# One of four additions of the negated row maxima, in an attention that runs beside another layer, put on GpSimd

## The chip, the cores and the metric

The kernel runs on one core of a Trainium2 chip. It is one launch, and the metric is the device time of that launch in microseconds. All arithmetic is float32. The engines are called by their short names: PE is TensorE (PEld its weight loads), DVE is VectorE, ACT is ScalarE, POOL is GpSimd and SP is SyncE. In this kernel every DMA of the main part is issued from SP.

## What is computed

The input is `x` of shape (4, 64, 64, 256). Layer 0 is a gated block: layernorm, a projection to 768 channels, two selective scans over 2x2 windows, a depthwise 3x3 convolution with a pointwise product, a gate, an output product, and a feed-forward part. Layer 1 is self-attention over the 4096 tokens of each of the four images:

```
f = xf @ Wf + bf
g = xf @ Wg + bg
hh = xf @ Wh + bh
scores = jnp.einsum('bnd,bmd->bnm', g, f)
attn = jax.nn.softmax(scores, axis=-1)
o = jnp.einsum('bnm,bmc->bnc', attn, hh)
o = o @ Wo + bo
out = gamma * o + xf
```

The change touches the softmax alone: the subtraction of the row maximum ahead of the exponential.

## The kernel before

**Two layers side by side.** Layer 0 is cut into 32 blocks of 512 tokens (4 images of 8 blocks). It runs alone until the first image is through (`until(NBLK - 1)`), since attention needs all keys and values of an image. From there on attention on the images that are ready runs beside the rest of layer 0, as Python generators whose pieces are interleaved by hand. `fill(RATE)` lets layer 0 advance by 7.2 "us" of the costs that its generators yield, and it is called once per step of attention. When layer 0 is through, the remaining queries are treated by other functions, `late_weights` and `attend_late`, which the change doesn't touch.

**Layer 0 on the vector engine.** The scan is most of it. For each direction and each of 8 states, L470 or L474 multiplies a PSUM bank (the transposed decays of L462) with SBUF data, L492 makes the next state from two SBUF tiles, and L485 adds to the output from two SBUF tiles. The convolution's taps (L595) and the layernorm (`layernorm`, L291 to L306) are on the vector engine too. Layernorm sends two small operations through GpSimd (L300, L301), and L303 waits for the second. In `tail` GpSimd adds a row of biases to `xo`, four times 128x256 (L660). These and a few memsets are all that GpSimd does.

**Attention beside it.** A block is 128 queries. `weights` makes its softmax weights in nine steps, each ended by a `yield`:

1. scores of half of the keys into four PSUM banks (L844), copied by ACT into two `eq` tiles of 128x1024 (L852);
2. the running maximum over them, DVE (L858, L860);
3. the scores of the other half, two more `eq` tiles;
4. the rest of the maximum (L860, L863);
5. two PE transposes, a DVE reduction with negation (L869), a PE transpose and an ACT copy (L873), which leave the negated maxima of the 128 queries in every partition of `nb`, 128x128;
6. to 9. for each of the four `eq` tiles `es[0]` to `es[3]`: an addition of `nb`, repeated eight times along the tile (L877), and an exponential in place on ACT (L878).

`attend` runs a block's products with the values, eight steps of four matmuls (L1036). In each step it advances `own` (the weights of its own block, if some are left), then `beside` (the weights of the next block), then layer 0. Eight steps advance `beside` through its steps 1 to 8, so step 9, the tile with `n == 3`, is left over: it is issued as `own` after the first step of the following `attend`. Step `k` of `attend` reads `es[k // 2]`, so `es[3]` is first read in step 6.

**Order.** A scheduler turns this order into one instruction stream per engine and puts in the semaphores. Each engine then works in the order of its own stream. The four `eq` tiles of a block come from a pool of six buffers, `nb` from a pool of two.

The lines concerned: the additions L877 and the exponentials L878; L873, which writes `nb`; L660, L300 and L301, which share GpSimd; L470, L474, L485, L492, L595, L860 and L303, which share the vector engine.

Of the kernel before, what the change touches and what calls it, by code (L numbers as in the profile page):

```python
# [23 lines left out]
ALU = mybir.AluOpType  # L24
# [4 lines left out]
P = 128  # L29
# [30 lines left out]
def block_then_attention_kernel(  # L60
# [18 lines left out]
    nc = tc.nc  # L79
# [85 lines left out]
    def behind(ins, last):  # L165

        if last is not None:
            tc.add_manual_dep(
                ins.ins, last.ins.name,
                mybir.DependencyInfo(mybir.DependencyClass.NoSync, mybir.DependencyReason.DATA), reason="side by side",  # L170
            )
        return ins
# [3 lines left out]
    def aside(shape=(P, TOK)):  # L176

        i = turn[0]
        turn[0] = (i + 1) % 4
        return pss.tile(list(shape), F32, tag=f"q{i}", name=f"q{i}")  # L180

    def four():

        return [
            pss.tile([P, TOK], F32, tag=f"q{i}", name=f"q{i}") for i in ((turn[0] - 1 - r) % 4 for r in range(4))
        ]
# [644 lines left out]
    def weights(b, q, es):  # L831


        fQ, gq = quarters[b], gqs.pop((b, q))
        mx = one.tile([P, TOK], F32, tag="mx", name="mx")
        for g in range(2):
            pr = four()

            with tc.high_priority():
                last = None  # L840
                for s in range(4):
                    at = g * TOK + s * P
                    for r in range(4):
                        ins = nc.tensor.matmul(  # L844
                            pr[r][:, s * P : (s + 1) * P], lhsT=fQ[CK * r : CK * (r + 1), at : at + P],
                            rhs=gq[CK * r : CK * (r + 1), :], start=True, stop=True,
                        )
                        last = behind(ins, last)
            for a in range(2):
                e = ep.tile([P, 2, TOK], F32, tag="eq", name="eq")  # L850
                for j in range(2):
                    nc.scalar.copy(e[:, j, :], pr[2 * a + j])  # L852
                es.append(e)
            yield
            for r in range(4):
                e = es[2 * g + r // 2]
                if g == 0 and r == 0:
                    nc.vector.tensor_tensor(mx, e[:, 0, :], e[:, 1, :], ALU.max)  # L858
                elif g == 1 or r > 1:
                    nc.vector.tensor_tensor(mx, mx, e[:, r % 2, :], ALU.max)  # L860
            if g == 0:
                yield
        nc.vector.tensor_tensor(mx[:, :QB], mx[:, :QB], mx[:, QB:], ALU.max)  # L863
        yield
        pm = aside()
        for c in range(2):
            nc.tensor.transpose(pm[:, c * P : (c + 1) * P], mx[:, c * P : (c + 1) * P], ident)
        nm = st.tile([P, 1], F32, tag="nm", name="nm")
        nc.vector.tensor_reduce(nm, pm[:, :QB], AX.X, ALU.max, negate=True)  # L869
        pn = aside()  # L870
        nc.tensor.transpose(pn[:, :P], nm.to_broadcast([P, P]), ident)
        nb = two.tile([P, P], F32, tag="nb", name="nb")
        nc.scalar.copy(nb, pn[:, :P])  # L873
        yield
        for n, e in enumerate(es):
            e8 = e.rearrange("p r (s q) -> p (r s) q", s=4)
            nc.vector.tensor_tensor(e8, e8, nb.unsqueeze(1).broadcast_to([P, 8, P]), ALU.add)  # L877
            nc.scalar.activation(e, e, AF.Exp)  # L878
            yield

# [180 lines left out]
    for n in range(4):  # L1061
        load_values(0, 0, n)
    es = []
    own = weights(0, 0, es)
    for _ in own:
        fill(RATE)
    a = 0
    while True:
        b, q = divmod(a, NQ)
        b1, q1 = divmod(a + 1, NQ)  # L1070
        if q1 == 0:
            until((b1 + 1) * NBLK - 1)
        ahead = []
        late = ready["tail"] == LAST - 1 and q1 % 2 == 0
        if late:
            n0 = (b1, q1 // 2)
            load_late_queries(*n0)
            beside = twice(late_weights(*n0, 0, ahead))
            attend(b, q, es, own, beside, lambda n: load_late_values(*n0, n))
            es = ahead  # L1080
            break
        if q1 == 0:
            quarter(b1, one, "fQ")
        load_queries(b1, q1)
        beside = weights(b1, q1, ahead)
        attend(b, q, es, own, beside, lambda n: load_values(b1, q1, n))
        es, own = ahead, beside
        a += 1
# [100 lines left out]
```

## Time and profile before

| what | value |
|---|---|
| runs (median of 3) | 5259.01 us (5250.38 to 5259.54) |
| the profiled execution | 5265.47 us |
| its span in the profile | 5263.6 us |
| granted TensorE clock, mean | 0.978 |
| layer 0 alone | until about 900 us |
| attention beside layer 0 | about 900 to 4330 us, 74 query blocks |
| attention alone (late functions) | about 4330 us to the end |
| L877 | 296 instructions, 357.4 us, 1220 ns each |
| GpSimd, all of it | 304 instructions, 204.0 us |

A block beside layer 0 takes about 47 us, so a step of `attend` takes about 6 us. The span of 5263.6 us is what the rows of the profile add up against. The profiled execution's own time is 1.9 us longer, and it lies 6.5 us above the median of the runs.

In the rows of the profile, "busy" is the time in which an engine executes, and "idle before" is how long the engine stood still just ahead of such instructions, with what ended the wait. Ends of matmuls are modelled, and spans on GpSimd are rough.

### The profile page before, as it was taken

Reading aid. Unit: us, or ns where it says so; the run is one execution under the profiler, and the core shown is the slowest. Engines: PE = TensorE matmul, PEld = TensorE weight load, DVE = VectorE, ACT = ScalarE, POOL = GpSimd, SP = SyncE. Lnnn points to the kernel's source line nnn. Section 1 sums busy time; section 2 is a strip of 40 time slices with the busy share of each in tenths; the row PEclk is TensorE's granted clock in tenths of the full one; section 3 lists DMA queues with packets and bytes.
Section 4 is the critical chain, followed back from the end, with each engine's and each line's share of the span. In section 5 each row is a group of like instructions: output and inputs, shape, how many; then the busy total and the mean of one; then the engine's idle time right before and its main releaser. Section 6 shows DMA issues by size and latency. Waiting matters only on the chain. (4 is left out here: it accounts for less than half of the span.)

```text
span 5263.6 us, 76327 instructions
## 1 busy us (share of the span) xinstructions
PE 4955.8 (94%) x27138; PEld 3543.4 (67%) x27138; DVE 4517.3 (86%) x8256; ACT 3571.5 (68%) x5489; POOL 204.0 (4%) x304
## 2 busy tenths in 40 slices
PE   7999998999999999999999999999999999999999
PEld 4565565666666666666666666666666667888887
DVE  7999999999899988998989988898989866666665
ACT  6778778667777767677777767777777635555554
POOL 0000000000000000000000000000000000000000
PEclk8999999999999999999999999999999999999999
DMA  1010011333333333334333333333333344444444
GB/s 48 26 44 19 23 34 34 102 122 115 118 104 119 113 109 115 114 116 118 118 111 106 119 108 111 118 114 118 112 116 104 112 129 146 147 147 147 147 147 139
DMA packets 330284, 554.14 MB, mean 105 GB/s; under 512 B 51504, under 2 KB 85936, under 8 KB 329904
## 3 DMA queue, kind: packets, MB, share of 16 engines
q1 hardware_dynamic: 326384, 545.40, 34.2%
q8 instruction: 214, 3.51, 0.3%
q10 hardware_dynamic: 3520, 3.87, 0.2%
q14 instruction: 166, 1.36, 0.1%
HBM read 490.28 MB, written 58.79 MB: 104 GB/s over the span
## 5 line engine op out<-in xcount | busy, mean ns | idle before, releaser
L1036 PE MATMUL acc<-vt,eq 128*128 128x257 f32 x4736 | 1215.4, 392 | 17.2 <-issue 7.6
L406 ACT ACTIVATE e<-dt,a_sc 128x384 f32<-128x384 f32 x1536 | 853.3, 611 | 272.8 <-PE bank L462 262.5
L1036 PEld LDWEIGHTS acc<-vt,eq 128*128 128x128 f32 x4736 | 875.0, 195 | 234.2 <-issue 107.6
L462 PEld LDWEIGHTS bank<-ident,e 128*128 128x128 f32 x4320 | 521.2, 143 | 319.5 <-issue 113.4
L462 PE MATMUL bank<-ident,e 128*128 128x128 f32 x4320 | 658.9, 279 | 79.1 <-DVE p L474 37.1
L1014 PE MATMUL bank<-vt,eT 128*128 128x257 f32 x2560 | 645.8, 382 | 0.0
L492 DVE SCALAR_TENSOR_TENSOR h<-u,bc,p 128x384 f32<-128x384 f32 x1024 | 613.4, 613 | 0.4
L485 DVE SCALAR_TENSOR_TENSOR y<-h,bc,y 128x384 f32<-128x384 f32 x960 | 589.0, 614 | 3.2 <-ACT y L483 0.4
L474 DVE TENSOR_TENSOR p<-bank,h 128x384 f32<-128x384 f32 x960 | 517.1, 548 | 55.1 <-PE bank L462 54.5
L1014 PEld LDWEIGHTS bank<-vt,eT 128*128 128x128 f32 x2560 | 478.6, 189 | 83.7 <-issue 13.9
L852 ACT COPY eq<-q 128x512 f32<-128x512 f32 x592 | 308.6, 587 | 192.6 <-PE q L844 117.5
L948 DVE TENSOR_TENSOR mx<-mx,eT 128x512 f32<-128x512 f32 x378 | 261.7, 692 | 152.2 <-ACT eT L943 121.3
L878 ACT ACTIVATE eq<-eq 128x1024 f32<-128x1024 f32 x296 | 308.1, 1053 | 103.0 <-DVE eq L877 100.1
L877 DVE TENSOR_TENSOR eq<-eq,nb 128x1024 f32<-128x1024 f32 x296 | 357.4, 1220 | 7.6 <-ACT nb L873 7.4
L595 DVE SCALAR_TENSOR_TENSOR ydw<-xp,vec,ydw 128x512 f32<-128x512 f32 x496 | 357.8, 743 | 1.4
L943 ACT COPY eT<-q 128x512 f32<-128x512 f32 x432 | 221.5, 597 | 194.7 <-PE q L935 194.7
L860 DVE TENSOR_TENSOR mx<-mx,eq 128x512 f32<-128x512 f32 x444 | 306.5, 690 | 38.4 <-ACT eq L852 31.5
L406 ACT ACT_TABLE_LOAD x241 | 309.2, 1283 | 14.4 <-PE bank L462 10.2
L485 DVE SCALAR_TENSOR_TENSOR y<-p,bc,y 128x384 f32<-128x384 f32 x512 | 313.1, 612 | 0.4
L470 DVE SCALAR_TENSOR_TENSOR p<-bank,bc,u 128x384 f32<-128x384 f32 x480 | 291.6, 608 | 21.1 <-PE bank L462 20.6
L973 DVE TENSOR_TENSOR eT<-eT,m 128x1024 f32<-128x1024 f32 x216 | 247.7, 1219 | 42.3 <-ACT m L970 42.3
L626 PE MATMUL q<-ydw,wpw 128*128 128x512 f32 x576 | 269.5, 602 | 13.3 <-ACT eq L852 12.8
(154 smaller groups left out, 7524.7 us busy)
## 6 DMA issues: line engine op xcount, KB each, us to landing
vt<-vod SPq DMA_DIRECT2D x1616, 257.0 KB, 2.8
vod<-vst SPq DMA_DIRECT2D x32, 514.0 KB, 3.9
xt<-in_x_dram SPq DMA_DIRECT2D x256, 64.0 KB, 1.9
xo<-in_x_dram SPq DMA_DIRECT2D x256, 64.0 KB, 2.3
x1d<-xo SPq DMA_DIRECT2D x32, 512.0 KB, 2.9
res<-x1d SPq DMA_DIRECT2D x74, 128.0 KB, 2.6
out_dram<-res SPq DMA_DIRECT2D x296, 32.0 KB, 1.6
fgd<-fg SPq DMA_DIRECT2D x32, 256.0 KB, 2.1
```

Source lines behind the costliest of these rows:

```text
L406: nc.scalar.activation(e[:, f, :], dts[d][:, f, lo : lo + 3 * P], AF.Exp, scale=a_sc[:, d, f * NST + n : f * NST + n + 1],)
L462: nc.tensor.transpose(pa[:, f * P : (f + 1) * P], es[d, n][:, f, off : off + P], ident)
L474: nc.vector.tensor_tensor(p, pa[:, :INNER], hs[d], ALU.mult)
L485: nc.vector.scalar_tensor_tensor(y[:, t, :], h, c, y[:, t, :], ALU.mult, ALU.add)
L492: nc.vector.scalar_tensor_tensor(hs[d], u[d][:, t, :], bc[:, t, d, n : n + 1], p, ALU.mult, ALU.add)
L595: nc.vector.scalar_tensor_tensor(o, x_tap, w_tap, o, ALU.mult, ALU.add)
L852: nc.scalar.copy(e[:, j, :], pr[2 * a + j])
L860: nc.vector.tensor_tensor(mx, mx, e[:, r % 2, :], ALU.max)
L877: nc.vector.tensor_tensor(e8, e8, nb.unsqueeze(1).broadcast_to([P, 8, P]), ALU.add)
L878: nc.scalar.activation(e, e, AF.Exp)
L1014: nc.tensor.matmul(sums[c][:, : DIM + 1], lhsT=e[:, r % 2, s, c * P : (c + 1) * P], rhs=vt[:, s, :], start=(n == 0 and s == 0), stop=(n == ...
L1036: nc.tensor.matmul(acc[:, : DIM + 1], lhsT=es[k // 2][:, k % 2, a : a + P], rhs=vt[:, s, :], start=(n == 0 and s == 0), stop=(n == 2 * NI ...
```

## The change

One line in the last loop of `weights`:

```diff
@@ -874,7 +874,9 @@
         yield
         for n, e in enumerate(es):
             e8 = e.rearrange("p r (s q) -> p (r s) q", s=4)
-            nc.vector.tensor_tensor(e8, e8, nb.unsqueeze(1).broadcast_to([P, 8, P]), ALU.add)
+            (nc.gpsimd if n == 3 else nc.vector).tensor_tensor(
+                e8, e8, nb.unsqueeze(1).broadcast_to([P, 8, P]), ALU.add
+            )
             nc.scalar.activation(e, e, AF.Exp)
             yield
 
```

For the fourth tile of each query block the addition of `nb` is issued on GpSimd. The three other additions stay on the vector engine, and all four exponentials stay on ACT. The 74 blocks make 74 such instructions. Operands, shapes and arithmetic are the same. The exponential of that tile waits for GpSimd's semaphore in place of the vector engine's. The additions of the late functions (L973) stay where they are.

## The prediction

> **What bounds the kernel now.** I read the page's shares first, then the busy times of the stage in which attention runs beside layer 0, then the chain of waits, then who waits for the additions, and last the order of instructions around an existing GpSimd addition.
>
> The page, engines and the two groups that the change touches:
>
> ```profile
> PE 4955.8 (94%) x27138; PEld 3543.4 (67%) x27138; DVE 4517.3 (86%) x8256; ACT 3571.5 (68%) x5489; POOL 204.0 (4%) x304
> ...
> L878 ACT ACTIVATE eq<-eq 128x1024 f32<-128x1024 f32 x296 | 308.1, 1053 | 103.0 <-DVE eq L877 100.1
> L877 DVE TENSOR_TENSOR eq<-eq,nb 128x1024 f32<-128x1024 f32 x296 | 357.4, 1220 | 7.6 <-ACT nb L873 7.4
> ```
>
> The stage alone, 860 to 4300 us (busy time of each engine):
>
> ```profile
> core 0: us, PE busy (x) PEld busy (x) DVE busy (x) ACT busy (x) POOL busy (x), PEclk, DMA share, GB/s
> 860.00:4300.00 3440.00, 3207.99 (x18191) 2280.67 (x18192) 3104.85 (x5734) 2448.27 (x3752) 148.77 (x216) 0.98 0.37 113
> ```
>
> In that stage PE is busy 93%, DVE 90%, ACT 71% and POOL 4%. PE and DVE bound it together, and neither has much room. The chain of waits, cut to 4100 to 4330 us, shows how they share it:
>
> ```profile
> by line: PE acc L1036 11.4%; PE q L626 7.6%; PE q L680 6.8%; DVE y L485 4.2%; PE q L704 3.0%; PE q L669 3.0%; PE q L844 2.7%; DVE eq L877 2.5%; DVE h L492 2.5%; DVE p L474 2.4%; ACT eq L852 2.3%; PE q L342 2.3%; PE q L649 2.3%; DMA vt<-vod
> ```
>
> L877 has 2.5% of these 230 us, 5.8 us, while its busy time between the same marks is 19.06 us: three tenths of it are on the chain. The page's chain goes back to about 4155 us only, so I followed the waits back in the same way from points spread over 1200 to 4300 us: PE has 51% of the way, DVE 27%, ACT 19%, and L877 some 78 us of its 356 us, 22%. A small saving or cost on DVE in this stage therefore reaches the end with 0.2 to 0.3 of its size.
>
> **What an addition on GpSimd does to DVE.** L660 is the same operation, 256 elements wide. POOL and then DVE around one group of them (start, duration):
>
> ```profile
> 1682.68 3.97 POOL L660 TENSOR_TENSOR xo<-xo,row 128x256 f32<-128x256 f32 x4 [0.53 <-DVE h L303]
> ```
>
> ```profile
> 1682.19 2.21 DVE L303 TENSOR_SCALAR h<-xo,mv,rstd 128x256 f32<-128x256 f32 x4 [1.47 <-POOL rstd L301]
> 1684.32 1.74 DVE L877 TENSOR_TENSOR eq<-eq,nb 128x1024 f32<-128x1024 f32 x1
> 1685.99 0.60 DVE L470 SCALAR_TENSOR_TENSOR p<-bank,bc,u 128x384 f32<-128x384 f32 x1
> 1686.52 0.54 DVE L474 TENSOR_TENSOR p<-bank,h 128x384 f32<-128x384 f32 x1
> ```
>
> L877, elsewhere 1217 ns, took 1.74 us: it stood 523 ns for one POOL addition of 256 elements. The third addition started at 1684.21 and the fourth, which waited behind L877, took 1.71 us. The same holds wherever the two meet: L485 and L492 read two SBUF tiles and go from 609 to 1080 ns, L860 from 684 to 1207 ns, L303 from 412 to some 815 ns. L470 and L474, which read one operand from PSUM, keep their 609 and 548 ns. [...]
>
> [...]
>
> **The change part by part.**
>
> *Removed from DVE:* 74 additions (296 / 4). From the start of the fourth addition of a block to the start of DVE's next instruction it is 1.13 us in the median, since the end overlaps the next start. 74 x 1.13 = 84 us. At the chain's 0.2 to 0.3 that is 17 to 25 us at the end; I take 22.
>
> *Added on POOL:* 74 additions of 1024 elements. Four times the 523 ns is 2.09 us [...]; I take 2.1. A record of 2.3 to 2.5 us follows from L660's 0.77 us plus three times 0.52 to 0.56. POOL has the time: 74 x 2.4 = 178 us beside its 204 us. Below nothing this cost cannot go.
>
> *When it starts:* POOL works in its own order and its queue is short, so the addition does not wait for DVE to come to that place. It goes as soon as `nb` is written (L873), on average 11 us before DVE began the fourth addition. In 15 of the 74 blocks a layernorm pair or an L660 group stands ahead of it in POOL's order and it starts some microseconds later, still before the exponential, which lies at 7 to 20 us after `nb` in the blocks that I looked at. Queued behind the addition are at most the two small layernorm operations, and L303 waits for those: 2.4 us of a 47 us block, so few of them, 4 us in all at most.
>
> *What DVE loses:* the time after `nb` is where DVE stands still least: 0.18 us in the first 4 us after `nb`, 0.02 in the next four, 0.19 in the third, per block. [...] With 2.1 us it is 1.86 us. 74 x 1.86 = 138 us. From both sides: 1.0 us each (74 us), if half of it fell on PSUM readers, to 2.2 us each (163 us).
>
> *On DVE in sum:* +138 - 84 = +54 us. How much reaches the end? A stall in one piece of 1.9 us eats up slack that many small ones wouldn't, and scan banks are three, so I give it 0.4, more than the chain's 0.27: +55 us. From 0.2 (28 us) to 0.8 (110 us).
>
> *ACT:* the fourth exponential stood 0.25 us on average for its addition, 74 x 0.25 = 18 us. That wait goes, since POOL is done early; at ACT's 19% of the chain, -4 us. What is late next is ACT's own queue, not the addition. PE reads `es[3]` in step 6 of the next `attend`, about 30 us later: covered.
>
> *Elsewhere:* no DMA is added or moved past another, L1036 and the late stage are the same instructions. The scheduler may place single instructions of other engines differently, and a place more or less between exponentials and other functions is a table load of 1283 ns on ACT; with ACT's share of the chain, ten more or fewer are 2 to 3 us.
>
> *Sum:* -22 + 55 - 4 = +29 us, cut to +25 for stalls that fall on DVE's idle 10%. Against the profiled execution, 5265.5 + 25 = 5290.5 us. It lies 6.5 us above the median of the runs shown, so against the median I say 5284 us.
>
> **The rivals.** The measurement can tell about 0.2% (10.5 us) from no change.
>
> *A, the forecast:* the addition blocks DVE longer than it relieves it. 5270 to 5330. [...]
>
> *B, faster:* the stall is hidden. Right after `nb`, PE stands still only 0.03 us in 4, so it has work that doesn't hang on DVE; if DVE regains the 1.9 us before PE needs a bank, only the saving remains: -22 - 4 = -26 us, 5233 us. It decides where less than 0.19 of the stall (26 / 138) gets through. Against it: DVE has hardly an idle moment for 12 us after that.
>
> *C, the two cancel:* 0.19 to 0.26 or so of the stall gets through[...]. 5259 us, within 10.
>
> *D, the whole net reaches the end:* DVE is the bound with all of its time, +54 us; with the stall counted whole and the saving at 0.3, +113. 5313 to 5370 us. Against it: PE has half the chain.
>
> *E, POOL late:* behind L300, waiting for a layernorm, the addition holds up ACT's queue. It would take more than the 15 places found, with each several us late; 5275 to 5300 us, and it is counted with A.
>
> **How the numbers follow.** A with E 0.52, D 0.12, C 0.15, B 0.21. So slower by over 0.2% is 0.64, within 0.2% 0.15, faster 0.21. The likeliest is A at 5284 us. For eight in ten the range must take in C, the upper part of B and the lower of D: 5240 to 5325 us. A's own range is 5270 to 5310 us.
>
> **What would show it.** In the changed kernel: 222 additions on DVE and 74 on POOL of 2.3 to 2.5 us (longer where they wait), starting within 2 us of `nb`; in those moments L485, L492, L860 or L877 of up to 2.8 us, and not L474; DVE's busy time up by about 50 us in spite of 74 instructions less; ACT's wait ahead of the fourth exponential gone; PE's waits for DVE at L462 longer. Wrong would be: DVE's two-input instructions unstretched, DVE's busy time down by 80 us, or a stretched DVE with a shorter span.

## The result, and the profile after

The changed kernel takes 5351.27 us (5348.35 to 5354.53, 4 runs) against 5258.53 us for the kernel before (also 4 runs). The ratio is 1.018, with a 95% interval of 1.0168 to 1.0193: 93 us slower. The forecast had the sign and a quarter of the size (25 us); the time lies above its range.

The page after, engines and the groups that the change touches:

```profile
PE 4972.9 (93%) x27138; PEld 3540.1 (66%) x27138; DVE 4580.5 (86%) x8182; ACT 3595.2 (67%) x5504; POOL 413.6 (8%) x378
...
L880 ACT ACTIVATE eq<-eq 128x1024 f32<-128x1024 f32 x296 | 308.3, 1054 | 186.2 <-POOL eq L877 95.6
...
L877 POOL TENSOR_TENSOR eq<-eq,nb 128x1024 f32<-128x1024 f32 x74 | 209.0, 2824 | 2014.4 <-ACT nb L873 1759.6
...
L877 DVE TENSOR_TENSOR eq<-eq,nb 128x1024 f32<-128x1024 f32 x222 | 333.1, 1512 | 6.2 <-ACT nb L873 6.0
```

DVE has 74 instructions less and is busy 63 us more. The additions that it kept take 1512 ns in place of 1220. ACT stood 103 us ahead of the exponentials (L878 before, L880 now), nearly all of it for their additions, and now stands 186, of which 96 for GpSimd. ACT also loads a function table 15 times more often (658 loads of 1283 ns against 643).

One block in both traces. Before, DVE and then ACT (start, duration, what they did, idle time ahead):

```profile
2017.80 3.50 DVE L877 TENSOR_TENSOR eq<-eq,nb 128x1024 f32<-128x1024 f32 x3 [0.85 <-ACT nb L873]
2021.21 0.68 DVE L684 TENSOR_TENSOR xo<-q,xo 128x512 f32<-128x512 f32 x1
```

```profile
2019.06 2.19 ACT L878 ACTIVATE eq<-eq 128x1024 f32<-128x1024 f32 x2 [1.29 <-DVE eq L877]
```

The same place in the changed kernel, POOL, DVE and ACT:

```profile
2050.46 3.40 POOL L877 TENSOR_TENSOR eq<-eq,nb 128x1024 f32<-128x1024 f32 x1 [7.20 <-ACT nb L873]
```

```profile
2050.41 5.66 DVE L877 TENSOR_TENSOR eq<-eq,nb 128x1024 f32<-128x1024 f32 x3 [0.85 <-ACT nb L873]
2055.99 0.68 DVE L684 TENSOR_TENSOR xo<-q,xo 128x512 f32<-128x512 f32 x1
```

```profile
2053.89 2.95 ACT L880 ACTIVATE eq<-eq 128x1024 f32<-128x1024 f32 x3 [3.51 <-POOL eq L877]
```

Three additions on DVE took 3.50 us and now take 5.66. Instruction by instruction they took 1.23, 3.38 and 1.21 us. DVE's first addition began 0.05 us ahead of GpSimd's, which took 3.40 us where the shortest of the 74 took 2.35. DVE's second one, with its 3.38 us, ended 1.07 us behind GpSimd's. So GpSimd seems to have stood for DVE's first addition, and DVE's second one for GpSimd. ACT, which began 1.29 us after going idle, now begins after 3.51 us. GpSimd's tile is exponentiated first here, not last.

Where PE felt it: the waits of the scan's transposes for banks that DVE has to release, before and after (total us, times, longest):

```profile
PE bank L462 <- DVE p L474: 37.1, 45, 2.5
PE bank L462 <- DVE p L470: 35.6, 28, 4.3
```

```profile
PE bank L462 <- DVE p L470: 63.5, 42, 4.1
PE bank L462 <- DVE p L474: 63.3, 60, 3.5
```

In all, PE stands still 72 us more (308 to 380 us). The other 17 us by which the two spans differ are PE's busy time (4955.8 to 4972.9 us); more of that below.

### The profile page after: what moved, and what is told of

Read it like the earlier page. It is cut to its first block, busy times and chain, and to the rows that moved or that the text cites. A ratio compares the mean times of both kernels' runs of the same rounds, so it can differ in the third digit from the quotient of the medians.

```text
span 5352.7 us, 76366 instructions
## 1 busy us (share of the span) xinstructions
PE 4972.9 (93%) x27138; PEld 3540.1 (66%) x27138; DVE 4580.5 (86%) x8182; ACT 3595.2 (67%) x5504; POOL 413.6 (8%) x378
## 4 chain that ended last, share of the span: by engine, by line
PE 44%; DVE 23%; ACT 13%; issue 2%; POOL 1%; DMA 0%; SPq 0%; POOLq 0%; DVEq 0%; ACTq 0%
PE bank L1016 11%; PE acc L1038 7%; PE acc L1016 4%; DVE y L485 4%; PE q L680 3%; DVE h L492 3%; ACT e L406 3%; DVE eq L877 3%; DVE ydw L595 3%; PE q L669 2%; DVE mx L860 2%; PE bank L462 2%; DVE p L474 2%; PE q L937 2%; ACT eq L852 2%
## 5 line engine op out<-in xcount | busy, mean ns | idle before, releaser
L492 DVE SCALAR_TENSOR_TENSOR h<-u,bc,p 128x384 f32<-128x384 f32 x1024 | 635.6, 635 | 0.7
L474 DVE TENSOR_TENSOR p<-bank,h 128x384 f32<-128x384 f32 x960 | 515.8, 546 | 58.1 <-PE bank L462 57.0
L880 ACT ACTIVATE eq<-eq 128x1024 f32<-128x1024 f32 x296 | 308.3, 1054 | 186.2 <-POOL eq L877 95.6
L877 POOL TENSOR_TENSOR eq<-eq,nb 128x1024 f32<-128x1024 f32 x74 | 209.0, 2824 | 2014.4 <-ACT nb L873 1759.6
L877 DVE TENSOR_TENSOR eq<-eq,nb 128x1024 f32<-128x1024 f32 x222 | 333.1, 1512 | 6.2 <-ACT nb L873 6.0
L860 DVE TENSOR_TENSOR mx<-mx,eq 128x512 f32<-128x512 f32 x444 | 306.3, 690 | 35.2 <-ACT eq L852 26.9
L406 ACT ACT_TABLE_LOAD x248 | 318.2, 1283 | 14.6 <-PE bank L462 10.3
L485 DVE SCALAR_TENSOR_TENSOR y<-p,bc,y 128x384 f32<-128x384 f32 x512 | 326.0, 637 | 0.2
L470 DVE SCALAR_TENSOR_TENSOR p<-bank,bc,u 128x384 f32<-128x384 f32 x480 | 291.1, 606 | 26.8 <-PE bank L462 25.9
```

The lines of the kernel that those rows point to most:

```text
L406: nc.scalar.activation(e[:, f, :], dts[d][:, f, lo : lo + 3 * P], AF.Exp, scale=a_sc[:, d, f * NST + n : f * NST + n + 1],)
L474: nc.vector.tensor_tensor(p, pa[:, :INNER], hs[d], ALU.mult)
L485: nc.vector.scalar_tensor_tensor(y[:, t, :], h, c, y[:, t, :], ALU.mult, ALU.add)
L492: nc.vector.scalar_tensor_tensor(hs[d], u[d][:, t, :], bc[:, t, d, n : n + 1], p, ALU.mult, ALU.add)
L877: (nc.gpsimd if n == 3 else nc.vector).tensor_tensor(e8, e8, nb.unsqueeze(1).broadcast_to([P, 8, P]), ALU.add)
```

## The experiments

Three theories were at hand. *Stall:* DVE stands while GpSimd adds, and nearly all of that reaches the end. *ACT:* the exponential that now stands first keeps ACT waiting. *Order:* the scheduler's new streams (one sequence of instructions per engine) are worse by themselves.

"Lost on DVE" below is worked out from each trace: over all DVE instructions that overlap a GpSimd addition of the experiment, the time above the median of the same instruction. In the changed kernel it is 141 us, 1.91 us per block. That DVE stands is measured; what in the hardware makes it stand, no run shows. Every time is given against runs of the kernel before on the same chip.

**e1, the exponentials kept in the order of the text.**

```diff
+        last = None
         for n, e in enumerate(es):
...
-            nc.scalar.activation(e, e, AF.Exp)
+            last = behind(nc.scalar.activation(e, e, AF.Exp), last)
             yield
```

> The changed kernel with one more edge of order: each exponential of a block stands behind the one before it in ACT's stream, so that the tile of GpSimd's addition is exponentiated last, as in the text, and not first. [...] it stays at 5335 to 5355 us, with DVE's busy time as in the changed kernel. ACT theory (the exponential now stands first and keeps ACT waiting for GpSimd, 96 us): 5285 to 5310 us, and ACT's wait for GpSimd gone.

5351.76 us, 91 us slower than before: ratio 1.0174 (1.0159 to 1.0189), no better than the change. ACT's waits for additions in this kernel:

```profile
ACT eq L881 <- DVE eq L878: 193.0, 92, 6.3
```

ACT no longer stands for GpSimd, but it stands as long for DVE, whose additions are held up by GpSimd. The ACT theory in its form "the wrong one stands first" falls. So does another suspicion: e1 has 641 table loads, two less than the kernel before, and is as slow as the change with its 658.

**e2, the stall alone.** `idle` is a tile of its own, 128x1024.

```diff
+            if n == 0:
+                s8 = idle.rearrange("p (s q) -> p s q", s=8)
+                nc.gpsimd.tensor_tensor(s8, s8, nb.unsqueeze(1).broadcast_to([P, 8, P]), ALU.add)
             nc.vector.tensor_tensor(e8, e8, nb.unsqueeze(1).broadcast_to([P, 8, P]), ALU.add)
             nc.scalar.activation(e, e, AF.Exp)
```

> The kernel before, with all four additions on the vector engine, and beside them one GpSimd addition per block, 128x1024, on a tile of its own that nobody waits for, begun when the negated maxima are there. The streams of DVE, ACT and PE are those of the kernel before. [...] DVE loses 74 times 1.9 us and no addition is saved, 5340 to 5385 us. ACT theory and the theory that the changed order alone costs: 5255 to 5290 us, since no wait and no order is changed.

5395.02 us, +134 us, ratio 1.0256 (1.0239 to 1.0273), 10 us above the range of the stall theory. Nobody waits for this addition, and DVE, ACT and PE work in the order of before. The exponentials and the additions in its page:

```profile
L883 ACT ACTIVATE eq<-eq 128x1024 f32<-128x1024 f32 x296 | 309.2, 1054 | 209.9 <-DVE eq L882 205.4
...
L882 DVE TENSOR_TENSOR eq<-eq,nb 128x1024 f32<-128x1024 f32 x296 | 417.2, 1421 | 8.0 <-ACT nb L875 7.6
```

DVE's additions go from 1220 to 1421 ns and ACT's wait for them doubles, from 100 to 205 us. Lost on DVE: 143 us, so 0.94 of it reach the end. The stall theory stands, and by itself it accounts for more than the whole result, since no addition is saved here.

**e3, GpSimd as long, but with fills; e4, nothing in its place.** Both leave out the fourth addition and keep e1's edge of order, and the streams of DVE, ACT and PE are those of e1. The edit of e3, against e1:

```diff
-            (nc.gpsimd if n == 3 else nc.vector).tensor_tensor(
-                e8, e8, nb.unsqueeze(1).broadcast_to([P, 8, P]), ALU.add
-            )
+            if n < 3:
+                nc.vector.tensor_tensor(e8, e8, nb.unsqueeze(1).broadcast_to([P, 8, P]), ALU.add)
+            else:
+                for _ in range(3):
+                    nc.gpsimd.memset(e, -1.0)
```

(e4 has no `else`.)

> As e1, but GpSimd fills the fourth tile three times (some 2.7 us) in place of adding: it writes and reads nothing, and the addition to that tile is left out. Streams of DVE, ACT and PE as in e1. [...] DVE isn't stretched, its busy time is 85 us under that of the kernel before, and the time is 5190 to 5245 us. If GpSimd's length or its semaphore is what costs: as e1. If the changed order costs: above 5270 us.

> As e1, but the fourth addition is left out altogether and GpSimd does nothing for it. Streams of DVE, ACT and PE as in e1. This is what 74 additions less on DVE are worth with the new order: 22 us by the prediction's step (5237 us), 60 us or more if DVE is the bound (5200 us). e3 should lie within 5 us of it unless GpSimd's waits matter.

e3: 5222.29 us, -38 us (0.9926, 0.9912 to 0.9941). e4: 5215.62 us, -45 us (0.9917, 0.9902 to 0.9931), between the two values expected. They are 7 us apart, where 5 were expected. GpSimd in e3, then the busy times of all engines in e4 and in e1:

```profile
L882 POOL MEMSET eq<- 128x1024 f32 x222 | 211.7, 954 | 2220.6 <-DVE mx L860 1823.2 <-PE q L342 133.0 <-PE q L626 84.2
```

```profile
PE 4920.9 (94%) x27138; PEld 3516.5 (67%) x27138; DVE 4440.9 (85%) x8182; ACT 3565.2 (68%) x5487; POOL 204.0 (4%) x304
```

```profile
PE 4972.6 (93%) x27138; PEld 3540.1 (66%) x27138; DVE 4581.8 (86%) x8182; ACT 3569.9 (67%) x5487; POOL 412.4 (8%) x378
```

GpSimd's fills are busy 212 us in e3, as long as the additions in the changed kernel (209 us), and DVE's busy time (4441.7 us) is within 1 us of e4's. So neither GpSimd's length nor its semaphore costs much (7 us), and these fills don't stretch DVE. (The fills begin behind the maximum, some time ahead of `nb`, so they don't test a wait at the changed kernel's moment.) Order falls as well: with e1's streams, which take the time of the changed kernel, the kernel is faster than before once GpSimd has no addition to make. From e4 to e1 the streams are the same and 136 us are added; e2 added 134 to the old streams. The parts add up: -45 + 134 = +89, and the change measured +93.

**Pauses and the clock.** PE's standing still is only part of these differences. From e4 to e1 the span grows by 134 us: PE stands still 83 us more, and it is busy 52 us more for the same 27138 matmuls. The granted clock falls from 0.985 to 0.976. The time lost to it, span times the missing share, is 78 us in e4 and 128 us in e1, so it grows by as much as the busy time. In e2 against the kernel before, the two parts are 95 and 33 us (clock 0.973 against 0.978). The traces of the kernel before and of the changed one record the granted clock at 1.00 or at 0.50: 47 stretches at 0.50 before, 235.7 us in sum, and 51 after, 254.3 us. One place in the changed kernel (stretch, its length, busy time of PE, PEld, DVE, ACT and POOL, granted clock, DMA share, GB/s):

```profile
2697.50:2700.91 3.41, 1.34 (x11) 0.93 (x9) 3.34 (x6) 2.88 (x8) 0.00 (x0) 1.00 0.29 77
2700.91:2704.32 3.41, 3.29 (x4) 1.50 (x5) 3.41 (x8) 3.39 (x7) 0.00 (x0) 0.50 0.00 0
```

Between 900 and 4250 us PE stood still for 57% of the 3.4 us ahead of a stretch at 0.50 in the kernel before and 60% in the changed kernel, against 7% and 8% of the whole time. In the kernel before, the 136 matmuls of L1036 inside such stretches took 635 ns in the median, those at 1.00 380 ns (ends modelled). So a stall that makes PE pause seems to cost a second time, in slower matmuls behind the pause. This is the author's estimate from these traces: no run varied the clock alone.

**What makes a stall cost its whole length?** The forecast had let 0.4 of it through. Four runs vary the kind, place and length of the loss. e5, e7 and e8 use an idle addition on GpSimd as e2 does, and keep the old streams. e5:

```diff
             if g == 1:
+                nc.gpsimd.tensor_tensor(idle, idle, e.rearrange("p r q -> p (r q)"), ALU.add)
```

> As e2 (kernel before, four additions on DVE, one idle GpSimd addition of 1024 elements per block), but GpSimd's addition reads the fourth tile of the following block's scores, and so begins when ACT has copied it, some 25 us after the negated maxima, where DVE stands still most. Streams of DVE, ACT and PE as in the kernel before. Theory of the place (the stall costs its whole length since it falls right behind the negated maxima, where DVE has no idle time and ACT waits for the first addition): 5295 to 5335 us, about half of e2's 134 us. Theory of the whole (a stall of DVE reaches the end nearly whole anywhere in the stage): 5370 to 5400 us.

e6 puts the loss on DVE as work:

```diff
+            if n == 0:
+                s8 = idle.rearrange("p (s q) -> p s q", s=8)
+                for m in (8, 6):
+                    nc.vector.tensor_tensor(s8[:, :m], s8[:, :m], nb.unsqueeze(1).broadcast_to([P, m, P]), ALU.add)
```

> The kernel before with two more additions on DVE per block, of 1024 and 768 elements on a tile of their own, ahead of the first addition of the negated maxima: about 2 us of DVE work per block, 148 us in sum, without GpSimd. The scheduler knows of them and sets the order anew. If DVE time is worth as much whichever way it is lost: 5370 to 5405 us. If a stall costs more than work, because the order was made without it: 5300 to 5350 us.

e7 is e2 with half the width (`[:, :4]` and 4 repeats):

> As e2, but GpSimd's idle addition is 512 elements wide. [...] If the cost goes with the held time: half of e2's stretch, about 0.9 us per block and 5320 to 5335 us. If slack swallows a short stall and only the part above some 1 us counts: 5265 to 5300 us.

e8 is e2 behind the fourth exponential:

```diff
             nc.scalar.activation(e, e, AF.Exp)
+            if n == 3:
+                nc.gpsimd.tensor_tensor(idle, idle, e.rearrange("p r q -> p (r q)"), ALU.add)
```

> As e2, but GpSimd's idle addition reads the fourth tile after its exponential, some 13 to 20 us behind the negated maxima: all four additions and exponentials are through by then, so that ACT's wait for the first one stays as before. Theory that ACT behind the stalled first addition carries the cost: 5270 to 5310 us. Theory of the whole: 5370 to 5400 us.

| run | time, us | against before | ratio (95%) | lost on DVE, us | share that reaches the end |
|---|---|---|---|---|---|
| e2, behind `nb` | 5395.0 | +134 | 1.0256 (1.0239 to 1.0273) | 143 | 0.94 |
| e7, the same, half as wide | 5316.3 | +57 | 1.0110 (1.0095 to 1.0125) | 65 | 0.88 |
| e5, while the next scores are copied | 5380.4 | +121 | 1.0231 (1.0216 to 1.0246) | 144 | 0.84 |
| e8, behind the exponentials | 5312.2 | +53 | 1.0104 (1.0087 to 1.0121) | 112 | 0.48 |
| e6, as DVE work ahead of the additions | 5338.5 | +80 | 1.0155 (1.0139 to 1.0170) | 152 (work) | 0.52 |
| e4, DVE work removed | 5215.6 | -45 | 0.9917 (0.9902 to 0.9931) | -85 (work) | 0.53 |

The share is the difference divided by the loss; for e4 and e6 the loss is the change in the sum of DVE's durations, and e4 has e1's streams besides. The difference holds PE's pauses and the clock together. e7 refutes that a short stall is swallowed: half the width costs near half, 57 of 134 us (4 us under the expected 5320). e5 refutes that only the moment behind `nb` is dear: there DVE stretches most at the running maximum (54 us of the 144; L864, L860 before), on the way to the next `nb`. e8, 2 us above its range for the cheap case, is cheaper on both counts: less is lost, since more of the scan's instructions that read PSUM fit in (27 us of GpSimd's additions, 13 in e2; beside the changed kernel's additions, L470 and L474 took 610 and 547 ns in the median, and 607 and 547 over the whole run), and half of that reaches the end. ACT's waits for the additions in e8 are those of the kernel before:

```profile
ACT eq L880 <- DVE eq L879: 101.4, 76, 4.2
```

So a stall on the way from scores to exponentials costs 0.84 to 0.94 of itself, and one behind it about half. That the place decides is read from e2, e5 and e8 alone, and part of the difference lies in the clock: against the kernel before, PE is busy 33 and 28 us more in e2 and e5 and 11 us less in e8, whose profiled run is its fastest. e6 does not fit the place: it stands on the same way as e2 and passes 0.52. The scheduler knows that work and made other streams for it. DVE's idle time shrinks by 65 us (746 to 681) where e2's shrinks by 15, but in e8, with the old streams, it shrinks by 69. What makes work cheaper than a stall wasn't separated.

**A better place for the addition?** In e9 to e12 GpSimd adds late, behind the third exponential of the block. e9 is the changed kernel with GpSimd's addition behind a small GpSimd operation that reads the third tile:

```diff
+            else:
+                seen = st.tile([P, 4], F32, tag="seen", name="seen")
+                gate_ = nc.gpsimd.tensor_scalar(seen, es[2][:, 0, :4], 0.0, None, ALU.mult)
+                behind(
+                    nc.gpsimd.tensor_tensor(e8, e8, nb.unsqueeze(1).broadcast_to([P, 8, P]), ALU.add), gate_
+                )
             nc.scalar.activation(e, e, AF.Exp)
```

> The changed kernel, but GpSimd's addition begins only when the third exponential of the block is through: a small GpSimd operation ahead of it reads that tile. [...] If the cost is the sum of what was measured by parts (45 us saved in e4, 53 us lost in e8): 5267 us, 5250 to 5285. If a stall of that length costs as in e2 and e5 once an exponential waits for it: 5335 to 5355 us.

> As e9, with two more yields between GpSimd's addition and the fourth exponential, so that ACT reaches it two steps later and cannot stand for GpSimd. If ACT's wait for the late addition carries part of e9's cost: 10 us or more under e9. If not: within 8 us of e9, as far as the other order that the scheduler makes costs nothing.

e9: 5313.96 us, +56 (1.0107, 1.0092 to 1.0122). e10: 5307.70 us, +50 (1.0092, 1.0076 to 1.0109). Both beat the change. e9 lies between its two expectations (5250 to 5285 and 5335 to 5355). ACT in e9 waited for the late addition:

```profile
ACT eq L885 <- POOL eq L883: 93.6, 48, 5.4
```

The two yields of e10 did not take that wait away (the fourth exponential still stood 0.98 us on average against 1.27), so e10 decides nothing. Two more runs tell more. e11 is e4 with the idle addition behind the third exponential, where nobody waits for it. e12 is e9 with one more yield and the fourth exponential put behind four score copies of the next block:

```diff
-            nc.scalar.activation(e, e, AF.Exp)
+            behind(nc.scalar.activation(e, e, AF.Exp), copied[-1] if n == 3 and len(copied) > 4 else None)
```

> As e4 (fourth addition left out), with an idle GpSimd addition of 1024 elements per block that reads the third tile after its exponential: [...] no exponential waits for GpSimd. Streams of DVE, ACT and PE as in e4. If the stall of DVE alone is the cost in e9: 95 us over e4, about 5310 us. If ACT's wait for the late addition (91 us in e9) carries half of it: 45 to 60 us over e4, 5260 to 5277 us.

> As e9, but the fourth exponential stands in ACT's stream behind the first four score copies of the following block, so that ACT doesn't stand for GpSimd. If ACT's wait carries part of e9's cost: 5260 to 5285 us. If the stall of DVE alone is the cost: 5300 to 5315 us.

e11: 5287.49 us, +31 (1.0057, 1.0041 to 1.0074). e12: 5285.59 us, +29 (1.0052, 1.0037 to 1.0067). Against e4's -45, e11 loses 76 us of 107 lost on DVE, e12 74 of 100, and e9 101 of 100. In e12 ACT's wait for GpSimd is down to 4 us from 94. So about 27 us of e9 were ACT's wait, as far as e12's other streams cost nothing, and the stall of DVE keeps a share of 0.7 in e11 and e12. e11's 76 us over e4 lie between its two expectations (45 to 60 and 95 us), and e12's time is 0.6 us above the upper edge of the cheaper case. No version with this addition on GpSimd beats the kernel before.

## Why the prediction was right or wrong

- **The DVE time removed** (84 us): right. In e4 the sum of DVE's durations falls by 85 us (its busy time, in which overlaps count once, by 76).
- **The record on POOL** (2.3 to 2.5 us, longer where it waits): right, 2.35 us at least, 2.82 on average.
- **When it starts** (as soon as `nb` is there): right, 0.26 us behind L873 on average. Seven blocks, not 15, began later than 0.5 us.
- **What DVE loses** (138 us; 1.86 per block of an estimated 2.1): right, 141 us, 1.91 per block. DVE's busy time was to rise by about 50 us and rose by 63. So DVE stood for one addition of 1024 elements about as the forecast had it from four times the 523 ns of 256 elements. Single additions on DVE took up to 3.4 us, where the forecast named 2.8.
- **How much of the stall reaches the end** (0.4, +55 us, with bounds of 0.2 and 0.8): this step failed. e2 and the pair e4 and e1 give 0.94 and 0.96, 134 and 136 us. The forecast scaled the share of DVE on the followed chain, 27%, up for a long stall; the share on one chain says how often an instruction is on it, not what 1.9 us at one place of every block do. The forecast also put the clock at nothing: between the spans of e4 and e1, 52 of 134 us are PE's longer busy time. And L877's share on the first chain was read too low: its 5.8 us were set against its busy time of 4100 to 4330 us (19.06 us), but that chain begins at 4154, and from there L877 is busy 14.2 us, so the share is four tenths and not three. The place was looked at only for DVE's and PE's idle time, not for what hangs on the held-up additions and maxima. Both bounds were too low.
- **The saving** (22 us of 84): too small as well, 45 us in e4 (with e1's streams; between the spans, 35 of 51 us are less busy time of PE, at a higher clock). With the measured shares, 0.53 and 0.94, the forecast's own 84 and 138 us would have given -45 + 130 = +85.
- **ACT's wait for the fourth exponential goes** (-4 us): wrong. The scheduler put that exponential first in 47 of 74 blocks, and ACT's waits for additions rose by 83 us. e1 shows that the place of the exponential cost nothing: ACT stands for DVE's stalled additions in its stead.
- **The rivals.** The time lies in the range of D, the stall counted whole, 5313 to 5370 us, which had 0.12. D's reason, that DVE is the bound with all of its time, is not what the runs show, since work taken off or put on DVE passes about half. B and C are refuted: hardly anything of the stall is hidden. E did not happen: GpSimd's addition began 2.5 us behind L873 at the most. A was given two upper ends, 5330 and 5310 us; the result lies above both.

DVE's stretch by additions and not by fills held in each run that tests it: DVE lost 143 us to GpSimd's additions in e2, and its busy time in e3 is within 1 us of e4's.

## What to carry to other kernels

Before moving an elementwise operation from DVE to GpSimd, count the time in which DVE will stand for GpSimd against the time that it saves, and only then look at idle time on GpSimd. Here each move freed 1.15 us of DVE and cost it 1.91 us, and still 1.34 us where more PSUM readers fitted in (e12). Price a stall by what waits for the instruction that it hits, and not by its engine's share of the chain: here 0.84 to 0.94 of it reached the end on the way to the exponentials, 0.5 to 0.7 behind it. Look at the granted clock too: from e4 to e1 PE paused 83 us more and was busy 52 us more for the same matmuls, at a clock of 0.976 in place of 0.985. A moved instruction may also let the scheduler reorder its consumers, so read the streams before counting on "it is done long before it is needed".

## What the hardware showed that was not expected

Three fills of 128x1024 on GpSimd (954 ns each) left L492, which reads two SBUF tiles, at its length (614 ns in e3, 613 before), while one addition of the same tile, 2.35 us at the least, cost DVE 1.91 us per block. The loss grows with the width without a visible fixed part that matters: 65 us for 512 elements (e7), 143 us for 1024 (e2).
